# Column products on 64x128 tiles for half of the inverse stage of a convolution and wavelet kernel

## The chip, the cores and the metric

The kernel runs on one core of a Trainium2 chip. Its time is the device time of one launch in microseconds (us). A time of before is given as the median of three runs. TensorE is called PE here, its weight loads PEld, VectorE DVE, ScalarE ACT, GpSimd POOL, and SyncE, which issues the DMAs, SP.

## The reference

The input is 4 x 64 images (batch x channels) of 256 x 256 in float32. Four layers follow each other. Cut to what matters:

```python
def conv(x, hx, hy, bias):            # layers 0, 2 and 3; hx, hy: a small network's output, [C, 256]
    k = hx[:, :, None] * hy[:, None, :]              # a separable filter for each channel
    y = causal_2d_convolution(x, k)                  # by rfft2 with zero padding to 512, cropped to 256
    return y + x * bias[:, None, None]

def mix(x, v, conv_w, tau):           # layer 1
    f1 = haar2d(x); acc = 0
    for i in range(2):
        f4 = einsum('bchw,oc->bohw', f1 * v[i], conv_w[i])
        acc += sign(f4) * relu(abs(f4) - tau[i])
    return haar2d(acc, inverse=True) + x

out = conv(conv(mix(conv(x, ...), ...), ...), ...)
```

The filter is an outer product, so each convolution is two one-dimensional ones: one along the rows and one along the columns.

## The kernel before

The kernel holds an image as four blocks of 64 rows. An item is four images in a tile of [128 partitions, 8, 256]: each half of the partitions has two images side by side, one after the other four blocks of 64 rows. On entry the half is the batch image and the place within it is the channel. There are 64 items in two groups of 32 (`GROUPS * ROUNDS`); a group is one half of the batch.

Three stages follow each other, and each overlaps the next. Phase A does layer 0 and the forward Haar transform for all 64 items. Phase B does the channel mixing and the threshold of layer 1, once for each group. Phase C does the inverse Haar transform and layers 2 and 3 for all 64 items.

A one-dimensional convolution is a product with a triangular Toeplitz matrix, and `toeplitz` (L289 to L300) issues it. The stationary operand is a 64 x 64 block of the image, and the moving operand is a stretch of filter values, of which block `k` needs only the first `N - 64 k` columns: 256, 192, 128 and 64. One call makes the 64 output rows of one block `j` for all four images of an item. For each `k` it issues four matmuls, one for each of four 64 x 64 tiles of the array: `r` is the partition half that is read, and also picks the PSUM bank `ps[r]`; `c` is the image within that half, and picks the half of the output partitions. So a call is 16 matmuls. A float32 matmul is two passes on PE, each with a weight load and a MATMUL, so a call is 32 MATMULs and 32 weight loads in the trace.

Each convolution in phase C is four calls of `rows` (L826) and four of `columns` (L838). The product leaves each image transposed, so that two of them in turn are a row and a column convolution; it also swaps the roles of `r` and `c`, so that between `rows` and `columns` the partition half is the channel. In `rows`, ACT copies each finished PSUM bank to the tile `ch` (L836), with image `r` as one run of 4 x 256 values for a partition, and `columns` reads `ch` as its stationary operand. The filter that `columns` moves (`filters_y`) therefore depends on the partition half `r` alone; the one of `rows` (`filters_x`) differs between the two images of a half. After `columns`, DVE adds the input times the bias to each bank (L855). In the profile the products carry the names of their PSUM tiles: `c1r` and `c1c` are rows and columns of layer 2, `c2r` and `c2c` of layer 3. `c0ps` is the last step of the inverse Haar transform (L305), `f` the channel mixing of phase B (L603).

The order on every engine is written out by hand. Phase C is a list of pieces, 18 for an item: four `rows` of one layer, half of the Haar product of the next item, four `columns` of layer 3 of the item two before, four `rows` of layer 3 of the item before, the other half of the Haar product, and four `columns` of layer 2. Copies and additions wait in a list (`later`) and are issued by the next piece (`flush`). `beside` lays phase B's second group into phase C's pieces in proportion:

```python
main = c_first + a_end[:1] + c[:BLOCKS] + c[mid:C_PIECES] + a_end[1:] + c[BLOCKS:mid] + c[C_PIECES:cut_c]
beside(main, phase_b(1), len(c_first) + len(a_end) + 2 * BLOCKS, 0)
...
beside(c[cut_c:], [], 0, 0)
```

So items 0 to 28 of phase C run beside phase B, and the rest run alone. `alone` (L734) is 32, the first item of the second group; from there on a part of the threshold is done in phase C.

Of the kernel before, what the change touches and what calls it, by code (L numbers as in the profile page):

```python
# [48 lines left out]
B, C, N = 4, 64, 256  # L49

ROW = 64
BLOCKS = N // ROW
# [44 lines left out]
def conv_haar_kernel(  # L97
    ctx: ExitStack, tc: tile.TileContext, x, zT, w1, wbd, cols, wo, decay, wo_first, decay_first, bias, forward, inverse, wrow, pack, v, v_rows, out
):
    nc = tc.nc  # L100
# [21 lines left out]
    def big(tag, name, bufs):  # L122
        return ac.tile([P, 2 * M, N], F32, tag=tag, name=name, bufs=bufs)

    def blocks(images):

        return images.rearrange("p (i k) j -> p i k j", i=2)
# [4 lines left out]
    def banks(name):  # L132

        ring = rings[asked[0] % len(rings)]
        asked[0] += 1
        return [ring.tile([P, 2, N], F32, tag="ps", name=f"{name}_{r}") for r in range(2)]
# [147 lines left out]
    TILES = [(r, c) for r in range(2) for c in range(2)]  # L284

    def half(r):
        return slice(r * ROW, (r + 1) * ROW)

    def toeplitz(ps, data, t, j):  # L289

        for k in range(BLOCKS):
            for r, c in TILES:
                nc.tensor.matmul(  # L293
                    ps[r][half(c), j % 2, k * ROW :],
                    data[half(r), c, k, bass.ts(j, ROW)],
                    t(r, c)[:, : N - k * ROW],
                    start=k == 0,
                    stop=k == BLOCKS - 1,
                    tile_position=(r * ROW, c * ROW),
                )  # L300

    def haar(ps, pairs, matrix):

        for r, c in TILES:
            nc.tensor.matmul(  # L305
                ps[r][half(c)].rearrange("p h k -> p (h k)"),
                matrix[half(r)],
                pairs(r, c).rearrange("p h k -> p (h k)"),
                start=True,
                stop=True,  # L310
                tile_position=(r * ROW, c * ROW),
            )

    def filters_x(toep):
        return lambda r, c: toep[half(r), c * PERIOD : c * PERIOD + N]

    def filters_y(toep):
        return lambda r, c: toep[half(r), CI * PERIOD :]
# [72 lines left out]
    def later(op):  # L391

        waiting.append(op)
# [23 lines left out]
    def phase_a():  # L417
# [13 lines left out]
        def rows(t, j):  # L431
            s = st[t]
            if j == 0:
                s["y"] = big("t0", f"ay_{t}", 2)
            if j % 2 == 0:
                s["ps"] = banks(f"a1ps{j}_{t}")
            toeplitz(s["ps"], blocks(s["x"]), filters_x(s["toep"]), j)
            if j % 2:
                for r, ps in enumerate(s["ps"]):
                    y = blocks(s["y"])[:, r, j - 1 : j + 1]  # L440
                    later(lambda y=y, ps=ps: nc.scalar.copy(y, ps))  # L441

        def columns(t, j):
            s = st[t]
            if j == 0:
                s["x1"] = big("m0", f"x1_{t}", 2)
            if j % 2 == 0:
                s["ps2"] = banks(f"a2ps{j}_{t}")
            toeplitz(s["ps2"], blocks(s["y"]), filters_y(s["toep"]), j)
            if j % 2:  # L450
                for e, ps in enumerate(s["ps2"]):
                    later(lambda e=e, ps=ps: residual(t, e, j, ps))
            if j == BLOCKS - 1:
                s["fw"] = big("m1", f"fw_{t}", 2)
                s["ops"] = forward_free(s["x1"], s["fw"], f"f{t}_")
# [274 lines left out]
    def phase_c():  # L730
# [3 lines left out]
        alone = total - ROUNDS  # L734
        st = [dict() for _ in range(total)]

        def load(t):
            if t >= total:
                return
            st[t]["g"] = big("in", f"g_{t}", 3)  # L740
            st[t]["scales"] = scales(st[t]["g"])
            for rows, g in all_rows(mixed[t // ROUNDS], t % ROUNDS, st[t]["g"], False):
                nc.sync.dma_start(g, rows)

        def load_raw(t):
            if alone <= t < total:
                r = st[t]["raw"] = late["sb"].tile([P, 2 * M, N], F32, tag="raw", name=f"raw_{t}", bufs=2)
                for rows, to in all_rows(unshrunk, t % ROUNDS, r, False):
                    nc.sync.dma_start(to, rows)
# [76 lines left out]
        def rows(t, l, j):  # L826
            s = st[t]
            if j == 0:
                s["half", l] = big("t0", f"ch{l}_{t}", 2)
            if j % 2 == 0:  # L830
                s["ps", l] = banks(f"c{l}r{j}_{t}")
            toeplitz(s["ps", l], blocks(s["y"]), filters_x(s["toep", l]), j)
            if j % 2:
                for r, ps in enumerate(s["ps", l]):
                    y = blocks(s["half", l])[:, r, j - 1 : j + 1]
                    later(lambda y=y, ps=ps: nc.scalar.copy(y, ps))  # L836

        def columns(t, l, j):  # L838
            s = st[t]
            if j == 0:  # L840
                s["new"] = big("out", f"o_{t}", 2) if l == 2 else big("m0", f"cy_{t}", 2)
            if j % 2 == 0:
                s["ps", l] = banks(f"c{l}c{j}_{t}")
            toeplitz(s["ps", l], blocks(s["half", l]), filters_y(s["toep", l]), j)
            if j % 2:
                new, old = blocks(s["new"]), blocks(s["y"])
                for e, ps in enumerate(s["ps", l]):
                    later(lambda e=e, ps=ps: residual(t, l, e, j, new, old, ps))
            if j == BLOCKS - 1:
                s["y"] = s["new"]  # L850

        def residual(t, l, e, j, new, old, ps):
            at = l * C + t % ROUNDS * CI + e
            to, of = new[:, e, j - 1 : j + 1], old[:, e, j - 1 : j + 1]
            nc.vector.scalar_tensor_tensor(to, of, bias_sb[:, at : at + 1], ps, ALU.mult, ALU.add)  # L855
            if l == 2 and t == total - 1:

                nc.sync.dma_start(blocks(out[t // ROUNDS, t % ROUNDS])[:, e, j - 1 : j + 1], to)
# [10 lines left out]
        def piece(t, j):  # L869
# [23 lines left out]
            if R1 <= j < R1 + BLOCKS:  # L893
                if t < total:
                    rows(t, 1, j - R1)
            elif C2 <= j < C2 + BLOCKS:
                if 1 < t:
                    columns(t - 2, 2, j - C2)
            elif R2 <= j < R2 + BLOCKS:
                if 0 < t <= total:  # L900
                    rows(t - 1, 2, j - R2)
            elif j >= C1:
                if t < total:
                    columns(t, 1, j - C1)
            else:
                product(t + 1, int(j > BLOCKS))
# [183 lines left out]
```

## Time and profile before

| what | value |
|---|---|
| median of 3 runs | 2596.64 us (2595.73 to 2599.01) |
| profiled execution, own time | 2597.8 us |
| its span, first to last instruction | 2595.7 us |
| mean granted PE clock | 0.979 |
| PE busy | 2343.0 us (90%), 53292 MATMULs |
| DVE, ACT, POOL busy | 1800.2, 1325.6, 2025.0 us |
| first `c1r` and first `c2c` | 1121.4 and 1189.7 us from the start |
| last `f` (end of phase B) | 1875.5 us |
| last `c2c` | 2591.1 us |

Busy times are of one execution, and the engines overlap, so they don't add up to the span. A busy PE counts from the start of a MATMUL to its modelled end, and several tiles of the array can work at once: the mean duration of one MATMUL times their number is far more than the busy time of the group.

### The profile page before, as it was taken

What the parts mean: (1) busy time and instruction counts of PE and PEld (TensorE: products, weight loads), DVE (VectorE), ACT (ScalarE), POOL (GpSimd) and SP (SyncE); (2) the same over time, 40 slices, a digit from 0 to 9 for tenths busy, and PEclk for the clock granted to TensorE, in tenths of its full rate; (3) what the DMA queues carried; (4) which work ended last, traced back from release to release, by engine and by line L of the source; (5) the groups of instructions that cost most, each with busy time, mean ns of one, the idle gap of its engine ahead of it and who ended that gap; (6) DMA issues with size and microseconds to landing.
All of it is one profiled execution on the core that took longest, in us unless ns stands there. A gap on an engine that the chain in (4) does not pass through costs nothing.

```text
span 2595.7 us, 118630 instructions
## 1 busy us (share of the span) xinstructions
PE 2343.0 (90%) x53292; PEld 1915.7 (74%) x53292; DVE 1800.2 (69%) x2049; ACT 1325.6 (51%) x2187; POOL 2025.0 (78%) x2428
## 2 busy tenths in 40 slices
PE   5999999788888888768999999999989999999999
PEld 4887877444444444547777877788889999999998
DVE  2555445799999999646666666666658777777773
ACT  1221112566666666226666665666655655655552
POOL 1898887899999999757657666766679999999991
PEclk8999999899999999979999999999999999999999
DMA  7676897699999999556989888888776666666653
GB/s 209 222 242 231 289 311 281 245 347 317 343 330 328 347 319 335 180 194 214 333 302 315 317 303 302 306 304 311 275 224 203 220 208 215 214 220 207 220 165 113
DMA packets 203678, 685.25 MB, mean 264 GB/s; under 512 B 29289, under 2 KB 30826, under 8 KB 190755
## 3 DMA queue, kind: packets, MB, share of 16 engines
q1 hardware_dynamic: 203171, 677.67, 75.8%
q8 instruction: 418, 6.85, 1.1%
q14 instruction: 89, 0.73, 0.1%
HBM read 427.93 MB, written 249.63 MB: 261 GB/s over the span
## 4 chain that ended last, share of the span: by engine, by line
PE 59%; DVE 13%; DMA 8%; POOL 8%; issue 5%; ACT 3%; SPq 2%; DVEq 0%; ACTq 0%; POOLq 0%
PE c2c L293 10%; PE c2r L293 9%; PE c1c L293 9%; PE c1r L293 9%; PE a1ps L293 6%; PE a2ps L293 5%; PE f L603 4%; PE c0ps L305 4%; DMA v<-in_v 3%; DVE x L622 3%; POOL fw L341 3%; POOL f L343 2%; DVE a L639 2%; DVE m L644 2%; PE a3ps L305 2%
## 5 line engine op out<-in xcount | busy, mean ns | idle before, releaser
L293 PEld LDWEIGHTS a2ps<-toep,ay 64*64 64x64 f32 x8192 | 313.2, 138 | 161.7 <-DVE f L474 85.0
L382 POOL TENSOR_TENSOR i<-i,g 128x16 f32<-128x16 f32 x744 | 398.3, 556 | 27.7 <-ACT g L359 0.6
L293 PE MATMUL a2ps<-toep,ay 64*64 64x128 f32 (+3 forms) x8192 | 360.1, 307 | 50.8 <-DVE f L474 42.4
L603 PE MATMUL f<-ft,mix 64*64 64x512 f32 x2048 | 312.0, 619 | 95.6 <-DVE x L622 80.2
L293 PEld LDWEIGHTS c2c<-toep,ch 64*64 64x64 f32 x8192 | 314.6, 134 | 59.0 <-ACT ch L836 25.9
L293 PEld LDWEIGHTS a1ps<-toep,x 64*64 64x64 f32 x8192 | 293.8, 134 | 83.8 <-issue 43.1
L293 PE MATMUL a1ps<-toep,x 64*64 64x64 f32 (+3 forms) x8192 | 338.8, 300 | 15.3 <-issue 12.3
L293 PEld LDWEIGHTS c1c<-toep,ch 64*64 64x64 f32 x8192 | 313.3, 134 | 51.6 <-ACT ch L836 26.6
L662 POOL TENSOR_TENSOR gt<-m,ft 128x512 f32<-128x512 f32 x128 | 163.6, 1278 | 236.3 <-DVE m L644 230.7
L293 PE MATMUL c1r<-toep,z 64*64 64x128 f32 (+3 forms) x8192 | 324.4, 299 | 21.5 <-issue 11.6
L293 PE MATMUL c2c<-toep,ch 64*64 64x192 f32 (+3 forms) x8192 | 328.7, 300 | 11.8 <-ACT ch L836 8.7
L293 PEld LDWEIGHTS c1r<-toep,z 64*64 64x64 f32 x8192 | 303.9, 134 | 46.6 <-issue 22.2
L293 PE MATMUL c1c<-toep,ch 64*64 64x128 f32 (+3 forms) x8192 | 324.3, 299 | 11.1 <-ACT ch L836 10.4
L382 POOL TENSOR_TENSOR ci<-i,g 128x1024 f32<-128x1024 f32 x124 | 318.2, 2586 | 4.5
L293 PE MATMUL c2r<-toep,cy 64*64 64x128 f32 (+3 forms) x8192 | 318.4, 298 | 2.9 <-issue 2.7
L293 PEld LDWEIGHTS c2r<-toep,cy 64*64 64x64 f32 x8192 | 301.4, 134 | 24.7 <-issue 13.3
L441 ACT COPY ay<-a1ps 128x512 f32<-128x512 f32 x256 | 137.4, 589 | 353.6 <-PE a1ps L293 353.0
L628 ACT ACTIVATE m<-x 128x1024 f32<-128x1024 f32 x194 | 206.3, 1063 | 194.2 <-DVE x L622 87.6
L639 DVE TENSOR_TENSOR a<-a,v 128x1024 f32<-128x1024 f32 x192 | 236.3, 1231 | 49.0 <-ACT a L634 48.9
L836 ACT COPY ch<-c2r 128x512 f32<-128x512 f32 x256 | 137.5, 591 | 247.1 <-PE c2r L293 246.6
L634 ACT ACTIVATE a<-x 128x1024 f32<-128x1024 f32 x194 | 199.6, 1029 | 109.4 <-DVE m L644 109.4
L855 DVE SCALAR_TENSOR_TENSOR cy<-z,bias_sb,c1c 128x512 f32<-128x512 f32 x256 | 176.9, 742 | 109.5 <-PE c1c L293 109.5
(80 smaller groups left out, 3869.2 us busy)
## 6 DMA issues: line engine op xcount, KB each, us to landing
toep<-filt SPq DMA_DIRECT2D x384, 224.0 KB, 5.3
ft<-coef SPq DMA_DIRECT2D x128, 512.0 KB, 7.4
v<-in_v SPq DMA_DIRECT2D x64, 1024.0 KB, 9.4
mixed<-gt SPq DMA_DIRECT2D x128, 512.0 KB, 7.5
g<-mixed SPq DMA_DIRECT2D x256, 256.0 KB, 5.7
x<-in_x SPq DMA_DIRECT2D x128, 256.0 KB, 4.7
coef<-f SPq DMA_DIRECT2D x128, 256.0 KB, 4.2
x<-in_x SPq DMA_DIRECT2D x32, 1024.0 KB, 7.8
```

Source lines behind the costliest of these rows:

```text
L293: nc.tensor.matmul(ps[r][half(c), j % 2, k * ROW :], data[half(r), c, k, bass.ts(j, ROW)], t(r, c)[:, : N - k * ROW], start=k == 0, stop=k ...
L305: nc.tensor.matmul(ps[r][half(c)].rearrange("p h k -> p (h k)"), matrix[half(r)], pairs(r, c).rearrange("p h k -> p (h k)"), start=True, s ...
L341: nc.gpsimd.tensor_tensor(diffs, even, odd, ALU.subtract)
L382: engine.tensor_tensor(to, s, d, op)
L441: later(lambda y=y, ps=ps: nc.scalar.copy(y, ps))
L603: nc.tensor.matmul(un[u]["f4"][half(q), b, :], mixers[0][half(r), bass.ts(i, C)], st[s]["f"][half(r), b], start=True, stop=True, tile_posi ...
L628: nc.scalar.activation(un[u]["m"], un[u]["x"], AF.Sign)
L634: nc.scalar.activation(un[u]["a"], un[u]["x"], AF.Abs)
L639: nc.vector.tensor_tensor(un[u]["a"], un[u]["a"], both(u, "tau"), ALU.subtract)
L662: nc.gpsimd.tensor_tensor(g[:, 0], m[:, 0], st[s]["f"][:, 0], ALU.add)
L836: later(lambda y=y, ps=ps: nc.scalar.copy(y, ps))
L855: nc.vector.scalar_tensor_tensor(to, of, bias_sb[:, at : at + 1], ps, ALU.mult, ALU.add)
```

## The change

For items of the first group (`t < alone`, 32 of 64) `columns` calls a new function, `toeplitz_wide`. For `k` = 0 and 1 (256 and 192 moving columns) it issues two matmuls instead of four: each takes the blocks of both images of a partition half, side by side, as one stationary operand of 64 rows and 128 columns, and fills all 128 output partitions of its bank. For `k` = 2 and 3 it issues the four 64 x 64 matmuls of before. For this the two images must lie beside each other in `ch`, so a new function `turn` writes ACT's copy in runs of 64 values at a distance of 128 instead of one run of 512. The `rows` products, the second group, phases A and B and the order of the pieces stay as they are.

```diff
+    def side_by_side(data):
+
+        return data.rearrange("p n k -> p (n k)").rearrange("p (k j c q) -> p k j c q", k=BLOCKS, j=BLOCKS, c=2)
+
+    def toeplitz_wide(ps, data, t, j):
+
+        for k in range(BLOCKS):
+            both = k < BLOCKS // 2
+            for r, c in [(0, slice(0, 2)), (1, slice(0, 2))] if both else [(r, slice(c, c + 1)) for r, c in TILES]:
+                nc.tensor.matmul(
+                    ps[r][c.start * ROW : c.stop * ROW, j % 2, k * ROW :],
+                    data[half(r), k, j, c].rearrange("p c q -> p (c q)"),
+                    t(r, 0)[:, : N - k * ROW],
+                    start=k == 0,
+                    stop=k == BLOCKS - 1,
+                    tile_position=(r * ROW, c.start * ROW),
+                )
+
+    def turn(data, r, j, ps):
+
+        to = side_by_side(data)[:, j - 1 : j + 1, :, r]
+        nc.scalar.copy(to, ps.rearrange("p i (j q) -> p i j q", q=ROW))
...
                 for r, ps in enumerate(s["ps", l]):
+                    if t < alone:
+                        later(lambda r=r, ps=ps: turn(s["half", l], r, j, ps))
+                        continue
                     y = blocks(s["half", l])[:, r, j - 1 : j + 1]
...
-            toeplitz(s["ps", l], blocks(s["half", l]), filters_y(s["toep", l]), j)
+            if t < alone:
+                toeplitz_wide(s["ps", l], side_by_side(s["half", l]), filters_y(s["toep", l]), j)
+            else:
+                toeplitz(s["ps", l], blocks(s["half", l]), filters_y(s["toep", l]), j)
```

## The prediction

> **What bounds the kernel now.** I read the page's busy row first, then the chain that ended last, then the busy times of two stretches, then the waits in the first of them. PE is busy for 90% of the span, and 59% of the chain is PE work:
>
> ```profile
> PE 2343.0 (90%) x53292; PEld 1915.7 (74%) x53292; DVE 1800.2 (69%) x2049; ACT 1325.6 (51%) x2187; POOL 2025.0 (78%) x2428
> PE 59%; DVE 13%; DMA 8%; POOL 8%; issue 5%; ACT 3%; SPq 2%; DVEq 0%; ACTq 0%; POOLq 0%
> ```
>
> The change touches items 0 to 31 of phase C, so the stretch beside phase B (1210 to 1870 us) is what counts. Against it stands the second group (1960 to 2560). The columns are busy us of PE, PEld, DVE, ACT and POOL with their counts, then granted clock, DMA share and GB/s:
>
> ```profile
> 1210.00:1870.00 660.00, 619.52 (x14127) 517.35 (x14123) 413.13 (x435) 405.45 (x711) 440.83 (x524) 0.99 0.87 307
> 1960.00:2560.00 600.00, 599.26 (x16387) 570.30 (x16383) 448.85 (x485) 338.86 (x629) 539.99 (x540) 1.00 0.63 203
> ```
>
> PE is busy for 619.5 of 660 us, and the next engine, POOL, for 440.8. The chain of this stretch has 81.5% on six PE groups, 4.9% "issue", 3.5% on the DMA of `g`, and 1.4% or less on any DVE line. So PE sets the pace here, and time added to PE's stream is added to the end, but for what falls into PE's own waits. PEld's largest waits in the stretch:
>
> ```profile
> PEld c1r L293 <- issue: 20.7, 36, 3.0
> PEld c1c L293 <- ACT ch L836: 17.0, 25, 2.1
> PEld c2c L293 <- ACT ch L836: 15.2, 29, 1.9
> PEld c2r L293 <- issue: 12.2, 38, 1.5
> PEld c2c L293 <- issue: 11.1, 27, 1.5
> ```
>
> "issue" means that nothing shown held PE. These waits are absent from the second group, where the DMA share is 0.63 and not 0.87; I take them for instructions that arrive late.
>
> **What streaming costs.** In phase B's mixing, four 64x64 tiles with 512 columns each take 0.43 us from their first start to the next group's:
>
> ```profile
> 1437.61 0.64 PE L603 MATMUL f<-ft,mix 64*64 64x512 f32 x4
> 1438.04 1.51 PE L293 MATMUL c2r<-toep,cy 64*64 64x256 f32 x36
> ```
>
> That is 0.84 ns a column with all four tiles at work at once, and no time between two groups on 64x64 tiles. So a round of 256 columns is 0.216 us, of 192 0.162, of 128 0.108, of 64 0.054, and a call is 2 x 0.54 = 1.08 us. The layer-0 network puts passes of 256 columns on a wide stationary operand of 128 columns: its four passes end 1.13 us after their start, where the first alone has 0.48, so (1.13 - 0.48)/3 = 0.217 us a pass. **A wide pass streams no faster than four narrow ones beside each other.** Two wide tiles (r = 0 and 1) do in 0.216 us what four narrow ones did; the change saves no streaming. This step assumes that two wide tiles run side by side, which no row of before shows.
>
> **What changing the tiles costs.** The Trainium skill, "TensorEngine Tiling (Array Packing)", section Tiling Modes, Key Properties, says that changing the tiling mode, rather than the tile, drains TensorE. The trace of before agrees: the network's matmuls stand between 64x64 products of phase A. With narrow windows that isolate the last narrow MATMUL, the first wide one, and what follows:
>
> ```profile
> 34.87 0.22 PE L293 MATMUL a1ps<-toep,x 64*64 64x64 f32 x1
> 35.02 0.48 PE L190 MATMUL mlp_ps<-z_sb,w_sb 33*128 33x256 f32 x1
> ...
> 35.02 1.13 PE L190 MATMUL mlp_ps<-z_sb,w_sb 33*128 33x256 f32 x4
> 36.08 0.66 PE L293 MATMUL a1ps<-toep,x 64*64 64x256 f32 x8
> ...
> 152.54 0.38 PE L192 MATMUL mlp_ps<-h,wbd_sb 128*128 128x256 f32 x1
> 152.85 0.43 PE L293 MATMUL a2ps<-toep,ay 64*64 64x256 f32 x1
> ```
>
> *Narrow to wide:* from the last narrow start, 34.87, to the wide start, 35.02, pass 0.15 us, where a 64-column round takes 0.054; and the first wide MATMUL takes 0.48 us against 0.38 for a later one (152.54). So about 0.10 for the array to empty and 0.10 for weights that could not be loaded ahead: 0.20. *Wide to narrow:* 35.02 + 0.10 + 4 x 0.217 = 35.99, and the narrow one starts at 36.08: 0.09 for emptying; its first MATMUL takes 0.43 against 0.38: 0.05 for weights. Together 0.14. The skill's "TensorE: Matmul & The Clock Gate", section LDWEIGHTS, prices a load at columns/1.2 ns: 107 ns for 128 columns, 53 for 64, which the 0.10 and 0.05 confirm. That this is no semaphore wait follows from its sameness: the pieces at 35, 99 and 152 us all take 1.06 us from the first wide start to the next narrow one, although the waits view puts the 0.33 us of idle PEld ahead of the latter once on "issue" and once on DVE.
>
> **The sum.** A `columns` call goes from narrow (other work, or k = 3 of the call before) to wide (k = 0, 1) and back (k = 2, 3). There are 32 items x 2 layers x 4 = 256 calls.
>
> - Added: 256 x (0.20 + 0.14) = **+87 us** on PE, in order ahead of everything else that PE does.
> - Removed: 4 matmuls, so 8 MATMULs and 8 weight loads a call; 2048 of each. Streaming: 0, as above. Their gain can only be in late instructions: 4.9% of 660 is 32 us, and some 34 in the 690 us from the first `c2c` (1190) to the end of phase B. PE's instructions there fall by some 14% (2048 of 14127 x 690/660 = 14770) and are spread over more time. I take a little under half, **-15**; the ends are 0 and -34.
> - Hidden: where a call waits for ACT's `ch` anyway (25 + 29 waits) the array is already empty: 54 x 0.09 = **-5**. In the first three items PE is not yet the bound (51.7 us busy of 80 from 1100 to 1180): half of 24 calls x 0.34 = **-4**. PE's waits for POOL's `ci` (5.1) and DVE's `x` (3.6) take up part of the delay: **-4**.
> - Uneven tiles: the timeline shows the tiles of neighbouring groups interleaved (at 1416 us `f` and `c2r`), so some tiles finish earlier than others, and at a change of tiles they stand idle for the slowest. Not shown by itself: between 0 and 0.10 us a call (0 to +26); I take 0.03, **+8**.
> - ACT's copy writes the same 512 values for a partition, in eight runs of 64. No row of before has that form. Its bound is 0 to 10% of the 591 ns; the chain has 0.9% of the stretch on ACT's `ch`, 6 us, so at most 0.6 us counts. 0.
> - Nothing moves past a DMA or on SP or POOL; in the built program the list of waits of every engine is that of before. The PE list has 1024 matmuls of 128 columns in place of 2048 of 64, so the change does what it says.
>
> Sum: 87 - 15 - 5 - 4 - 4 + 8 = **+67 us**. The profiled execution took 2597.8 us (its span is 2595.7), so 2665; the median of the runs lies 1.2 lower: **2664 us**. After phase B nothing gives it back: in the second group PE is busy for 599.3 of 600 us. Nothing is late in DVE or ACT that was not: they wait for PE (DVE 86.0 us for `c2c`, ACT 85.4 for `c1r` in the stretch), and wait longer.
>
> **Rivals.**
>
> 1. *Faster: no emptying between 64x64 and 64x128.* Both split the rows in two, and if PE could load a wide operand behind narrow work, the change would cost nothing and keep only the relief in late instructions, -15 to -34: about 2575 us. It decides below 15/256 = 0.06 us a call. For it: the stalls exist, exactly in the first group. Against it: the network's `33*128` operand also needs no more than 64 rows, and shows the same 1.06 us as the full `128*128`. 6%.
> 2. *Much slower: the two wide tiles run in turn.* Then the rounds of k = 0 and 1 double: 2 x (0.216 + 0.162) = 0.76 us a call, 194 us more, 2858 us. Against it: four narrow tiles, two for each row half, do run at once. 4%.
> 3. *No change: PE has slack after all,* and the delay falls into waits of its own. PE's idle time in the stretch is 40.5 us of 660, so even all of it (42 in 690) leaves 87 - 42 = 45; another engine would have to be the bound, and the next is at 440.8 of 660. 3%.
>
> **From this to the numbers.** A measurement of this kernel can tell about 0.2% (5 us) from no change. The likeliest case (87%) gives 2664. Its low end is 87 - 34 - 13 - 6 for more hidden = +34, 2631; its high end 87 + 26 - 5 = +108, 2705. The range 2632 to 2702 holds nearly all of it, and leaves the rivals out. Faster 0.06 (rival 1), same 0.03 (rival 3), slower 0.91.
>
> **What would show it.** In the profile of the changed kernel: 2048 fewer MATMULs (53292 to some 51244); groups of 64*128 for `c1c` and `c2c` whose first MATMUL of a call is about 0.10 us longer than the later ones; PE gaps of about 0.1 us at each change of tiles; end of phase B near 1940 instead of 1875 us, and the second group as long as before. The prediction is wrong if a call beside phase B takes less than 0.2 us more than before, if the wide groups start without the longer first MATMUL (rival 1), or if a call takes over a microsecond more (rival 2). "issue" in the chain should shrink but not vanish.

## The result and the profile after

The changed kernel takes 2646.25 us (median of 4 runs, 2645.37 to 2647.54) against 2597.71 us of the kernel before in the same comparison. The medians differ by 48.5 us. The ratio is 1.0177, with a 95% interval of 1.0155 to 1.0200; in us this is 46, and 40 to 52. So the kernel is slower, and the 48.5 us that are used below are known to some 6 us. The span of the profiled execution is 2644.3 us, 48.6 more than before.

The page of the changed kernel: busy time and instructions of each engine, and the DMA queue that the page calls "instruction" (packets, MB, share of the 16 DMA engines).

```profile
PE 2416.4 (91%) x51244; PEld 1839.7 (70%) x51244; DVE 1811.5 (69%) x2049; ACT 1325.4 (50%) x2187; POOL 2021.3 (76%) x2428
...
q8 instruction: 402, 6.59, 1.0%
```

PE has 2048 MATMULs fewer (53292 - 51244), and is busy for 73 us more. DVE, ACT and POOL do what they did, to within 12 us.

Four narrow windows of the changed kernel's PE timeline: the first pass of k = 0 on the two wide tiles, its second pass, the first narrow MATMULs (k = 2), and the start of the next call (start, time, group, count):

```profile
1259.69 0.49 PE L311 MATMUL c2c<-toep,ch 64*128 64x256 f32 x2
...
1260.01 0.38 PE L311 MATMUL c2c<-toep,ch 64*128 64x256 f32 x2
...
1260.65 0.34 PE L311 MATMUL c2c<-toep,ch 64*64 64x128 f32 x4
...
1261.14 0.49 PE L311 MATMUL c2c<-toep,ch 64*128 64x256 f32 x2
```

This is one call with nothing else in it: from the first wide start to the next call's, 1261.14 - 1259.69 = 1.45 us. The same stretch of the kernel before, for a call of 32 MATMULs on 64x64 tiles, in two windows (the second begins with the next call):

```profile
1438.04 1.30 PE L293 MATMUL c2r<-toep,cy 64*64 64x256 f32 x32
...
1439.13 0.59 PE L293 MATMUL c2r<-toep,cy 64*64 64x256 f32 x5
```

That is 1.09 us, so a call costs **0.36 us more**. It is not one lucky pair: between 1190 and 1900 us the trace has 102 wide calls with nothing between them and the next, with a median of 1.45 us, and the kernel before has 57 narrow ones, with a median of 1.09.

The first pass of both wide tiles together takes 0.49 us, where one MATMUL of it takes 0.48, so the two tiles run beside each other. From 1259.69 to the second pass 0.32 us go by, 0.10 more than a round of 256 columns (0.216): the weights that could not be loaded ahead, for PEld's first wide load starts at 1259.69, too. From there to the first narrow start 0.64 us go by, 0.10 more than the 0.216 + 2 x 0.162 = 0.54 us of streaming that is left: the array empties. The other 0.16 us of the price lie on the way back to the next wide start.

256 such calls are 92 us, but only 48.5 arrive. A good part of the rest shows in PE's own waits beside phase B (1210 to 1870 us; us in total, times, longest), first before, then after:

```profile
PE c1r L293 <- issue: 11.3, 11, 2.6
...
PE c2c L293 <- issue: 2.8, 3, 1.3
PE f L603 <- issue: 2.8, 5, 1.5
PE c2r L293 <- issue: 2.7, 4, 1.4
```

```profile
PE c1c L311 <- ACT ch L323: 4.5, 5, 1.1
PE c0ps L328 <- POOL ci L405: 3.8, 1, 3.8
...
PE c1r L293 <- issue: 0.7, 2, 0.4
```

The "issue" waits are 21.0 us before, with two more lines of 0.7 us each, and 0.7 us after. In PEld's list for the changed kernel a different kind stands under the same name, 38.7 us in 120 waits ahead of `c2c`: at about 0.3 us each these are probably the changes of tiles themselves.

Are these waits late instructions, as the prediction took them to be? The trace of the kernel before can say so, for it has the packets of the instruction queue, 16 KB each. All 25 "issue" waits of PE in the stretch end between 1.2 and 1.6 us after such a packet has landed; PE's 26 other waits there end anywhere from 0.1 to 8.5 us after one. So these waits end when instructions arrive.

The end of phase B (the last `f`) moved from 1875.5 to 1914.5 us, by 39. Of these, 4 us lie ahead of the first `c2c` (1189.7 to 1194.1), where `c1c` is wide already. The stretch after it grew from 720.2 to 729.8 us by the span. The last items of the first group run there, but not all of the 9.6 us are theirs: in the execution with the layout alone, below, this stretch has 724.1 us without one wide product.

### The profile page after: what moved, and what is told of

It is laid out like the page before. It is cut to its first block, busy times and chain, and to the rows that moved or that the text cites. A ratio compares the mean times of both kernels' runs of the same rounds, so it can differ in the third digit from the quotient of the medians.

```text
span 2644.3 us, 114534 instructions
## 1 busy us (share of the span) xinstructions
PE 2416.4 (91%) x51244; PEld 1839.7 (70%) x51244; DVE 1811.5 (69%) x2049; ACT 1325.4 (50%) x2187; POOL 2021.3 (76%) x2428
## 4 chain that ended last, share of the span: by engine, by line
PE 60%; DVE 13%; POOL 10%; DMA 7%; issue 5%; ACT 3%; SPq 1%; DVEq 0%; ACTq 0%; POOLq 0%
PE c2r L293 9%; PE c1r L293 8%; PE c2c L311 7%; PE c1c L311 6%; PE a1ps L293 6%; PE a2ps L293 6%; PE c2c L293 4%; PE c1c L293 4%; PE f L626 4%; PE c0ps L328 3%; POOL fw L364 3%; POOL f L366 3%; DVE x L645 2%; DVE a L662 2%; DVE m L667 2%
## 5 line engine op out<-in xcount | busy, mean ns | idle before, releaser
L626 PE MATMUL f<-ft,mix 64*64 64x512 f32 x2048 | 288.1, 618 | 90.0 <-DVE x L645 80.1
L293 PE MATMUL a1ps<-toep,x 64*64 64x128 f32 (+3 forms) x8192 | 339.4, 300 | 16.5 <-DMA x<-in_x 10.4
L293 PE MATMUL c1r<-toep,z 64*64 64x256 f32 (+3 forms) x8192 | 308.8, 298 | 12.4 <-ACT z L847 9.8
L293 PEld LDWEIGHTS c1r<-toep,z 64*64 64x64 f32 x8192 | 279.0, 134 | 51.9 <-issue 17.6
L293 PE MATMUL c2r<-toep,cy 64*64 64x256 f32 (+3 forms) x8192 | 307.7, 298 | 0.2 <-DMA toep<-filt 0.2
L884 DVE SCALAR_TENSOR_TENSOR o<-cy,bias_sb,c2c 128x512 f32<-128x512 f32 x256 | 177.2, 742 | 131.2 <-PE c2c L311 112.8
L497 DVE TENSOR_TENSOR f<-a3ps,wrow_sb 128x512 f32<-128x512 f32 x256 | 161.3, 682 | 131.5 <-PE a3ps L328 131.5
L645 DVE TENSOR_TENSOR x<-f,v 128x1024 f32<-128x1024 f32 x192 | 233.5, 1216 | 20.1 <-PE f L626 19.6
L667 DVE SCALAR_TENSOR_TENSOR m<-a,m 128x1024 f32<-128x1024 f32 x194 | 236.8, 1221 | 10.5
L364 POOL TENSOR_TENSOR fw<-x 128x1024 f32<-128x1024 f32 x64 | 122.7, 1918 | 153.2 <-DVE x L484 140.7
```

What stands on the lines that cost most here:

```text
L293: nc.tensor.matmul(ps[r][half(c), j % 2, k * ROW :], data[half(r), c, k, bass.ts(j, ROW)], t(r, c)[:, : N - k * ROW], start=k == 0, stop=k ...
L364: nc.gpsimd.tensor_tensor(diffs, even, odd, ALU.subtract)
L626: nc.tensor.matmul(un[u]["f4"][half(q), b, :], mixers[0][half(r), bass.ts(i, C)], st[s]["f"][half(r), b], start=True, stop=True, tile_posi ...
L645: nc.vector.tensor_tensor(un[u]["x"], un[u]["f4"], both(u, "v"), ALU.mult)
L667: nc.vector.scalar_tensor_tensor(un[u]["m"], un[u]["a"], 0.0, un[u]["m"], ALU.max, ALU.mult)
```

## The experiments

**Theory.** A round trip between 64x64 and 64x128 tiles costs some 0.36 us of PE, whatever the wide matmuls compute. Beside phase B a part of it is given back, since PE had waits there for instructions that came late, because the DMA engines were busy. **Rivals.** The wide matmuls or the new layout of `ch` cost the time; or the wide matmuls give something back wherever they stand, because they are fewer instructions.

Each of the comparisons has its own runs of the kernel before; the times below stand with the ratio to those.

### The layout alone

```diff
-            both = k < BLOCKS // 2
+            both = False
```

> The changed layout of ch alone: ACT writes it in runs of 64, and all columns products stay on 64x64 tiles. Theory (the change of tiles costs the time): as before, 2598 us within 0.2%, PE instructions 53292, late-instruction waits as before. Rival (the copy in short runs, or weights read from the new layout, costs part of the 48 us): 2605 us or more, and ACT's copy of ch longer than its 591 ns.

Measured: 2600.02 us, ratio 1.0003 (0.9991 to 1.0015). ACT's copy, from the view of tile `ch` (ns, least, median and most):

```profile
L323 ACT COPY ch<-c1r x128: 560/587/620, 1130.0 to 1944.0; 128x512 f32<-128x512 f32 x128
L862 ACT COPY ch<-c1r x128: 585/592/625, 1959.9 to 2568.1; 128x512 f32<-128x512 f32 x128
```

L323 is the copy in runs of 64, L862 the copy in one run of 512, in one execution: 587 against 592 ns. By the interval the layout costs 4 us at most, and the rival falls. PE's waits on "issue" beside phase B are 19.4 us, close to the 21.0 of the kernel before.

### The second group too

```diff
-                    if t < alone:
+                    if t < total:
                         later(lambda r=r, ps=ps: turn(s["half", l], r, j, ps))
...
-            if t < alone:
+            if t < total:
                 toeplitz_wide(...)
```

> Wide tiles in the second group too, so 512 calls of columns instead of 256. Theory: the first 256 calls cost 0.36 us each on PE and got some 26 us back from instructions that no longer arrive late and some 15 us from waits that were there anyway; the second group has neither, so its 256 calls cost 0.34 to 0.36 us each: 87 to 93 us more than the changed kernel, 2733 to 2739 us. Rival (fewer instructions or wide tiles themselves give something back wherever they are used): the second group costs no more than the first, 48 us, 2695 us.

Measured: 2730.18 us, ratio 1.0507 (1.0485 to 1.0530), 131 us over before. The second group's 256 calls add 131 - 48 = 83 us, 0.32 us each. In the second group PE is busy nearly all the time without this (599.3 of 600 us, in the prediction) and all the time with it:

```profile
2060.00:2660.00 600.00, 600.00 (x12612) 454.83 (x12602) 415.78 (x430) 303.86 (x563) 479.20 (x487) 1.00 0.58 182
```

12612 MATMULs in 600 us stand against 16387 before. About half of this fall is the change itself, for a wide call has 24 MATMULs where a narrow one has 32. An item of this group has 8 calls of `rows`, 8 of `columns` and 16 MATMULs of `c0ps`: 528 MATMULs before and 464 now. So 600 us hold 27.2 items instead of 31.0, 12% fewer, at a PE that counts as busy throughout: the modelled ends of the MATMULs cover the emptying of the array. The second group pays 83 us where the first paid 48, so the first does not owe its lower price to the wide matmuls. The price came out a little under the 87 that were expected; probably the calls that wait for `ch` find the array empty.

### Half the round trips

```diff
-                toeplitz_wide(s["ps", l], side_by_side(s["half", l]), filters_y(s["toep", l]), j)
+                for i in range(j // 2 * 2, j // 2 * 2 + 2):
+                    ks = range(BLOCKS // 2, BLOCKS) if j % 2 else range(BLOCKS // 2)
+                    toeplitz_wide(s["ps", l], side_by_side(s["half", l]), filters_y(s["toep", l]), i, ks)
```

`toeplitz_wide` goes over `ks` here, and the first matmul of an even block alone starts a bank, the last of the odd block closes it.

> The same matmuls on the same tiles, but k = 0 and 1 of two neighbouring blocks j together, then k = 2 and 3 of both: half the changes of tiles (one round trip for two calls). Theory: 128 round trips of 0.36 us fewer, 46 us, less a few that fell into waits: 2600 to 2610 us, and the late-instruction waits stay away. Rival (the wide matmuls cost the time, not the changes between tiles): 2646 us as in the changed kernel.

Measured: 2609.65 us, ratio 1.0041 (1.0028 to 1.0054). The same matmuls on the same tiles in another order win back 37 of the 48.5 us. The rival falls: it is the changes that cost. In the trace two paired calls with nothing else in them take 2.54 us, 0.36 more than two narrow ones (34 pairs, median). PE's waits on "issue" beside phase B stay away, with 1.4 us on `c1r`:

```profile
PE c1r L293 <- issue: 1.4, 2, 0.8
```

### All four products wide

```diff
-            both = k < BLOCKS // 2
+            both = True
```

> k = 2 and 3 wide as well. A run of four calls then changes tiles once, and once more for each f that falls into it (some 0.75): 1.75 round trips of 0.34 us, 0.60 us. But weights of 128 columns take 0.107 us, and a round of 64 columns streams in 0.054: 8 passes of k = 3 in a run cost 0.053 more each, 0.43 us. Theory: 1.03 us a run against 1.45 in the changed kernel, 64 runs: 27 us less, 2619 us. Rival (weight loads of 128 columns are hidden, or loads of the two row halves hinder each other): 2592 us in the first case, over 2650 in the second.

Measured: 2624.59 us, ratio 1.0097 (1.0079 to 1.0114), about 22 us under the changed kernel. 27 were expected. Fewer changes help, and loads of 128 columns that a short stream can't hide take part of it back. The 0.107 us in the expectation is the price of a load that the prediction gives with its source. Here a wide MATMUL of 64 columns has a mean of 247 to 249 ns where the narrow one has 218, and unbroken runs of four and of three wide calls (4.76 and 3.55 us from first to last start) are 1.20 us apart, where a narrow call takes 1.09: 0.11 us a call, or 0.45 for the four of a run where 0.43 were expected. Why 22 us came and not 27 is not shown.

```profile
L311 PE MATMUL c2c<-toep,ch 64*128 64x64 f32 x512 | 54.2, 247 | 0.0
```

### Less DMA traffic, without and with the change

```diff
+            if grp == GROUPS - 1 and s >= 8:
+                d["f"] = held[s % 4]
+                return
-            d["f"] = bp.tile(...)
+            d["f"] = held[s % 4] = bp.tile(...)
...
+            if grp == GROUPS - 1 and s >= 3:
+                d["v"], d["tau"] = kept[s % 3]
+                return
-            d["v"], d["tau"] = [], []
+            d["v"], d["tau"] = kept[s % 3] = [], []
```

> The kernel before, but phase B's second group loads v only for its first three steps and ft only for its first eight, and uses those tiles again afterwards, so the mixing of the later steps is of old data. That takes some 57 of 200 MB off the DMA of the stretch beside phase B. Theory (PE's unexplained waits there are instructions that come late because the DMA engines are busy): these waits, some 26 us, shrink to less than 10, and the time falls by some 20 us, to about 2578. Rival (the waits have to do with PE's own pattern of instructions and not with DMA traffic): the waits stay above 20 us, 2590 to 2598 us.

> The same loads left out of the changed kernel. Theory: it has no late instructions left to lose, so it stays at 2640 to 2646 us, and the difference to the light kernel without the change grows from 48 to 65 to 70 us, the change's cost without its relief. Rival: the difference stays near 48 us.

Both kernels leave loads out, so the later steps of phase B's second group mix old data; only their times are of use. Measured: 2573.51 us without the change, ratio 0.9891 (0.9875 to 0.9906), and 2647.37 us with it, ratio 1.0178 (1.0162 to 1.0193). Busy times, clock, DMA share and GB/s of the light kernel without the change, and the only "issue" line of PE in the same stretch:

```profile
1210.00:1870.00 660.00, 633.05 (x14735) 538.68 (x14731) 423.78 (x448) 418.86 (x741) 462.88 (x558) 0.99 0.65 228
```

```profile
PE c1r L293 <- issue: 0.6, 1, 0.6
```

With the DMA share at 0.65 instead of 0.87 the waits on "issue" are 0.6 us, and the kernel without the change is 27.6 us faster than before. PE's other waits in the stretch did not shrink (19.1 us before, 23.0 here), so the gain is not theirs. The packets of the instruction queue take a median of 1.0 us in both; what holds them back before they start is not shown. The changed kernel gains nothing: it had 0.7 us of these waits left.

So the change's price without this traffic is 2647.4 - 2573.5 = **74 us**, and the 25 us between 74 and 48.5 were paid back by waits that the DMA traffic makes. By the intervals these 25 are known to some 8 us. The other 92 - 74 = 18 us are a remainder: they hold what fell into waits that PE had anyway, and calls that cost less than the 0.36 us of a call with nothing else in it. At the 0.32 us of the second group the remainder would be 9.

### Only beside phase B

```diff
-                    if t < alone:
+                    if 3 <= t < 28:
```

(in `rows` and in `columns`, on the paired order)

> The paired order for items 3 to 27 alone, all of which lie beside phase B; the other items as before. Theory: the 26 round trips of the paired kernel outside that stretch bring no relief, so leaving them out gains 26 x 0.36 = 9 us: 2600 us, no different from before within 0.2%. Rival (the gap of the paired kernel to before lies in the stretch): 2609 us.

Measured: 2605.71 us, ratio 1.0020 (1.0011 to 1.0029), 5 us over before. The paired order for all items was 1.0041, 11 us. So some 6 of the expected 9 us came: the time lies between the two expectations. The interval still lies above 1, so this kernel is slower than the one before, by 3 to 8 us.

### A quarter of the round trips

In the same items, blocks 0 and 1 are paired and wide, blocks 2 and 3 on 64x64 tiles:

```diff
-            both = k < BLOCKS // 2
+            both = k < BLOCKS // 2 and j < 2
...
-                for i in range(j // 2 * 2, j // 2 * 2 + 2):
-                    ks = range(BLOCKS // 2, BLOCKS) if j % 2 else range(BLOCKS // 2)
+                for i in range(j // 2 * 2, j // 2 * 2 + 2) if j < 2 else [j]:
+                    ks = range(BLOCKS) if j > 1 else range(BLOCKS // 2, BLOCKS) if j % 2 else range(BLOCKS // 2)
```

> As the run before, but wide products for blocks 0 and 1 alone; blocks 2 and 3 on 64x64 tiles in the order of before. One round trip for a run of four calls: 50 instead of 100, 18 us less on PE. Theory 1 (the late instructions vanish as soon as PE has some of these breaks, so the relief stays): 2582 us, below before. Theory 2 (the relief goes with the number of instructions taken out, which is halved): 2595 us.

Measured: 2601.17 us, ratio 1.0001 (0.9992 to 1.0011). Both theories miss, the first by 19 us and the second by 6. The first falls: a part of the late instructions is back.

```profile
PE c1r L293 <- issue: 7.4, 8, 2.5
```

With 0.4 us on `c2r` these are 7.8 us, against 21.0 before and 1.4 for the paired order. 50 round trips at 0.36 us, 18 us, cost just what they take away. Against the paired order, this run halves the instructions taken out and also the breaks, so it does not say which of them counts. The next one does.

### Half the instructions, the same round trips

```diff
-            both = k < BLOCKS // 2
+            both = k == 0
```

> Wide products for k = 0 alone, k = 1 to 3 on 64x64 tiles: the same 256 round trips between tiles as in the changed kernel, but half as many instructions taken out (1024 MATMULs and as many weight loads). Theory (late instructions vanish because the breaks at the changes of tiles give the instruction stream time): the relief stays at some 26 us, 2646 us as in the changed kernel, and PE's waits on 'issue' beside phase B stay under 2 us. Rival (the relief goes with the number of instructions taken out): half of it, 2655 to 2660 us, and 7 to 12 us of those waits.

Measured: 2646.13 us, ratio 1.0190 (1.0164 to 1.0216), as slow as the changed kernel, and PE's wait on "issue" beside phase B is down to

```profile
PE c1r L293 <- issue: 0.3, 1, 0.3
```

With half as many instructions saved, nothing of the relief is lost. The run before it makes the comparison sharper. Between 1210 and 1870 us the two have the same number of wide weight loads, first a quarter of the round trips, then this run:

```profile
L311 PEld LDWEIGHTS c1c<-toep,ch 64*128 64x128 f32 x400 | 39.3, 187 | 28.7 <-ACT ch L323 22.1 <-ACT ch L862 2.9 <-ACT z L847 1.6
L311 PEld LDWEIGHTS c2c<-toep,ch 64*128 64x128 f32 x368 | 36.6, 186 | 25.0 <-ACT ch L323 21.6 <-ACT z L847 1.6
```

```profile
L311 PEld LDWEIGHTS c2c<-toep,ch 64*128 64x128 f32 x384 | 32.8, 186 | 46.4 <-ACT ch L323 22.9 <-issue 15.4 <-ACT z L847 2.4
L311 PEld LDWEIGHTS c1c<-toep,ch 64*128 64x128 f32 x384 | 31.8, 184 | 43.2 <-ACT ch L323 24.5 <-issue 13.8 <-ACT z L847 0.8
```

768 wide loads, and as many wide MATMULs, each in place of two narrow ones: both runs take out the same there. With 48 round trips 7.8 us of the waits stay; with 192, in every call and not in every fourth, it is 0.3 us. So the number of instructions taken out is not what brings the relief. It comes with the breaks.

Why a break helps is argued and not shown: PE may take no instructions while the array empties, so that those on their way catch up. A rival stands beside it, for a break also lowers the mean rate at which PE takes instructions: a call has 28 MATMULs in 1.45 us here, and 32 in 1.09 on 64x64 tiles. A run that slows PE evenly, without breaks, would tell the two apart; there is none.

No version beat the kernel before: with 0, 50, 100, 128 and 256 round trips in the first group the ratios are 1, 1.0001, 1.0020, 1.0041 and 1.0177. Up to some 100, late instructions and other waits pay for the breaks nearly in full, but not for more. The light kernel's 27.6 us are an estimate of what the late instructions cost in the kernel before; how to be rid of them without breaks was not tried.

## Why the prediction was right, point by point

- **PE sets the pace beside phase B: right.** Time on PE arrived at the end, and no other engine took it up. The third rival falls by the ratio of 1.0177.
- **No streaming saved: right.** The two wide tiles run side by side, and their later rounds take what rounds on four narrow tiles take (0.64 us from the second pass to the first narrow start, 0.10 of it for emptying). This step was an assumption, and the pair that is done within 0.49 us shows it. The second rival falls.
- **0.20 + 0.14 us a round trip: right.** 0.36 us were measured, with the uneven tiles in it: the four narrow tiles start one after the other, 0.02 us from the first to the last, which is the difference to 0.34. That is 5 us in 256 calls, where I had 8 (0.03). What the Trainium skill says in "TensorEngine Tiling (Array Packing)", Key Properties, that a change of mode drains TensorE, holds between 64x64 and 64x128, although both split the rows alike: 0.10 us pass before the first narrow start beyond the streaming. The first rival falls by this.
- **Late instructions, -15: too small, and for the wrong reason.** They gave back some 25 us, nearly all of what there was (21.0 us of waits beside phase B became 0.7), where I took under half of 34. This is the term that was furthest off. I had tied it to the 14% of instructions taken out; the runs with a quarter of the round trips and with k = 0 alone show that it comes with the breaks instead, be it for the pause or for the slower rate.
- **Hidden in other waits, -13: not settled.** The remainder is 18 us at 0.36 us a call and 9 at 0.32, with an error of some 6 us. -13 fits both.
- **The layout, 0: right** (1.0003).

The terms 87 + 5 - 25 - 18 give 49 us, but this is no test: 25 is 74 - 48.5 and 18 is 92 - 74, so the sum must close. What stands by itself are the 0.36 us of a call, the 21.0 us of waits that went, and the 74 us of the light pair. The point was 2664 us, 18 us high, of which the late instructions are some 10.

Of the signs that I had named, the 51244 MATMULs and the longer first MATMUL (0.48 us, 0.38 in the second pass) came as written, and "issue" fell from 4.9% to 2.1% of the chain in the stretch. The gaps of 0.1 us on PE did not show: the modelled ends reach over them. The end of phase B, which I had put near 1940 us, came at 1914.5: the late instructions gave back more, and some of the delay came only after it.

## What to carry to other kernels

Putting two small matmuls into one wide operand saved nothing here, because the small tiles already streamed side by side. It then cost a drain and an unhidden weight load at each change of tiles, and the number of changes, not of matmuls, was the bill. If both shapes are needed, put the work of one shape together first. An unexplained wait of PE next to a high DMA share is worth a look at the packets of the instruction queue and a run with less traffic before it is priced. Here a change that slowed PE seemed cheaper than it was, because it took such waits away.

## What the runs showed that was not expected

PE's waits on late instructions depend on the DMA traffic beside them: some 20 us at a DMA share of 0.87, 0.6 us at 0.65. Each of them ends some 1.4 us after a packet of the instruction queue has landed, which helps to tell them from other waits in a trace. They vanish also when PE has short breaks of its own: 256 breaks for 2048 and for 1024 saved MATMULs left 0.7 and 0.3 us. And PE counts as busy for 600.00 of 600 us in the kernel that is wide in both groups, while it gets through 12% fewer items in that time: breaks of 0.1 us don't show in its busy time.
